# Codes of the last part transposed by DMA, and loads and key parts moved to other tiles, in a quantized cross-attention and FFN kernel

## The chip, the cores and the metric

The kernel runs on one core of one Trainium2 chip. The metric is the device time of one execution in microseconds. Before the change it is 1822.46 us, the median of three runs (1821.18 to 1823.08).

## What is computed

One transformer block on 1600 query rows (16 x 100) of width 512, with a context of 5776 rows (16 x 361): normalized queries, 16 heads of width 32, keys, queries, values and attention weights rounded to 8-bit codes, then a gated FFN of width 1408 whose inputs are rounded row by row. Cut to what matters:

```python
# attention (x is layer-normalized first; B*N = 1600 rows, 5776 keys)
q = (x @ Wq + bq); k, v = split(cond @ Wkv + bkv)
q = fq_sym(q / sqrt(32), axis=-1); k = fq_sym(k, axis=-1); v = fq_sym(v, axis=keys)
attn = softmax(q @ k.T); attn = fq_unsigned(attn, axis=-1)     # codes 0..255 of the row's maximum
x = x + (attn @ v) @ Wp + bp
# FFN
xq = quant_input(layernorm(x))                                  # round(x * 127 / max|x|) per row
x1, x3 = split(xq @ w13.T)
inner = rmsnorm(relu(x1)**2 * x3) * norm_w
x = x + quant_input(inner) @ w2.T
```

## The kernel before

**Stages.** A prologue (to about 145 us) projects the queries, stores their codes in DRAM (`q_dram`) and makes the keys and values of the first four heads. Then come 200 steps, one for each pair of a head and a tile of 128 query rows (the 13th tile, 64 rows high, is shared by two heads, so two heads take 25 steps). Four heads make a group of 50 steps; groups are 0 to 3, and "step 1/35" below means tile 35 of group 1. The last part (from about 1567 us) is the FFN, tile of rows by tile of rows, 13 tiles.

**One step of the attention.** PE multiplies queries by 5776 keys in five chunks (L1247, or L1256 for the shared tile); DVE copies each chunk from PSUM to one of two `score` tiles and takes its maximum (L1263); POOL combines the maxima (L1295, L1306, L1307, which makes the bias `nb`); ACT takes the exponentials in two halves into codes (L1199: `pairc`, `codes`); two DMA transposes on SP's queue turn them (L1204 `pk`, L1207 `rT`); POOL unpacks the first half (L1220); PE multiplies by the values four steps later (L1126). In program order SP gets, in each step, first the `rT` of the step before, then loads, then its own `pk`.

**The plan.** All other work is put by hand into slots of a step with `put(n, slot, fn, ...)`: `pool` (first on POOL in the step), `turn` and `act0` (in one of the windows between chunks), `pe`, `late` (on POOL between the first and the second combination of maxima), `dve` and `act` (after the chunks). The tables `PLAN` (groups 0 to 2) and `LAST` (group 3) give the steps. "keys" holds, for each of the next heads and each part of eight key blocks, the step in which POOL splits it into three bf16 parts (`keys_split`, L368) and the step in which PE turns it (`keys_turn`, L390) and ACT copies it (`keys_keep`, L397); the second head of a group is needed first in step 12 (the shared tile), the third in 25, the fourth in 37 and the next group's first in 50. "query" holds the steps of the three loads of a head's query codes (`query_load`, L403), all three of which a score product needs. "weights" holds the loads and the scalings of four slices of `wp` (L771, L774).

**DMA queues.** Loads in the attention and all transposes are issued by SP; the loads and stores of group 3's partial projections, of the FFN weights (`piece_load`, L461), of `nw_b` (L846) and of the first two residual tiles (`a_load`, L862) by ACT. Each DMA counts on one of eight semaphores, given in turn to the DMAs of SP and ACT in program order.

**The last part.** `START` and then, for each tile t, `EACH` give the order. Each name is a function: `a_turn`, `a_project`, `a_norm`, `a_codes` (codes `hq` of the FFN's input), `a_keep` (four PE transposes into `ph`, one copy to `hT`), `b_up` (16 products for each of three chunks of the 1408), `b_relu`, `b_gate`, `b_codes` (codes `gq` of the inner activations), `b_turn` (eleven PE transposes into `pg` in two calls, copies to `gT`), `b_down` (22 products into `py`), `b_out`. In `EACH` the codes of tile t-1 are made at the start of iteration t, turned in its middle and multiplied in its second half; tile t+1 is prepared in the same iteration. `nw_b` (the norm's weights, 704 KB as they are spread over partitions), the residual tiles `x1_0` to `x1_3` and the other buffers of the last part lie in a ring of memory that in the attention holds the value codes, the key stacks and the queries and keys of the heads (`open_tail`, L829).

## Time and profile before

The profiled execution took 1828.33 us; its profile spans 1826.5 us.

| | us |
|---|---|
| median of the runs | 1822.46 |
| profiled execution, as timed | 1828.33 |
| its span | 1826.5 |
| PE busy | 1630.0 (89%) |
| DVE busy | 1701.5 (93%) |
| ACT busy | 1485.7 (81%) |
| POOL busy | 1321.6 (72%) |

DVE's largest group of instructions is the copy of scores with the maximum (L1263), 1000 times, 1302.1 us. The DMA engines moved 323.87 MB; 87.6% of 16 engines' span went to the queue of the transposes and SP's loads. Busy times are averages over stages; the stages have different limits, so a part of the change is read from its own stage.

In the profile, a row of a timeline gives its start, its duration (both in us), the engine (SPq and ACTq: the DMA issues of SP and ACT), the line, the operation, the tiles written and read, and in brackets the idle time before it and what ended that.

### The profile page before, as it was taken

To read this page: it belongs to the slowest core of one execution; us is meant where nothing else is said; L and a number is where in the kernel's file an instruction comes from. 1 tells how busy PE (TensorE), PEld (TensorE's weight loads), DVE (VectorE), ACT (ScalarE), POOL (GpSimd) and SP (SyncE) were. 2 spreads that over 40 slices of the span, in tenths; PEclk is the share of its full clock that TensorE was granted. 3 is DMA by queue.
4 is the path that set the end of the run, shared out by engine and by line. 5 is a ranking of instruction groups with operands and counts; after the bars stand their busy time and mean duration, and the time that the engine had idled before them with its cause. 6 is when DMAs were issued, how large, how long until landed. Compare 5 with 4: busy or idle time off the path is not lost. (4 is left out here: it accounts for less than half of the span.)

```text
span 1826.5 us, 43719 instructions
## 1 busy us (share of the span) xinstructions
PE 1630.0 (89%) x16745; PEld 1141.9 (63%) x16745; DVE 1701.5 (93%) x2939; ACT 1485.7 (81%) x1471; POOL 1321.6 (72%) x1852
## 2 busy tenths in 40 slices
PE   6999989988888998888889988898898999889998
PEld 6985666656565665565656655655555555568886
DVE  8889999999999998999999999999999999788886
ACT  4656999988899998888999988899889988654443
POOL 5557989877899887778898887889776756542221
PEclk9999999999999999999999999999999999989999
DMA  5646999999999999999999999999999999921000
GB/s 156 161 137 138 202 204 206 207 204 206 195 207 203 202 205 208 198 214 187 201 200 211 207 212 200 201 166 206 198 196 210 210 223 222 185 91 35 24 32 21
DMA packets 982447, 323.87 MB, mean 177 GB/s; under 512 B 939943, under 2 KB 946267, under 8 KB 982238
## 3 DMA queue, kind: packets, MB, share of 16 engines
q1 hardware_dynamic: 970380, 300.91, 87.6%
q10 hardware_dynamic: 11858, 20.18, 4.1%
q8 instruction: 131, 2.15, 0.5%
q14 instruction: 78, 0.64, 0.1%
HBM read 79.16 MB, written 10.72 MB: 49 GB/s over the span
## 5 line engine op out<-in xcount | busy, mean ns | idle before, releaser
L1263 DVE TENSOR_SCALAR_CACHE_REDUCE score<-sl 128x1536 f32<-128x1536 f32 (+1 forms) x1000 | 1302.1, 1354 | 51.8 <-PE sl L1247 35.1
L1247 PE MATMUL sl<-kT,qT 96*128 96x512 bf16 (+1 forms) x2304 | 633.0, 370 | 114.9 <-DVE score L1263 105.7
L1199 ACT ACTIVATE pairc<-score,nb,qs 128x2772 uint8<-128x2772 f32 x192 | 518.4, 2700 | 81.4 <-POOL nb L1307 62.3
L1199 ACT ACTIVATE codes<-score,nb,qs 128x3024 uint8<-128x3024 f32 x192 | 558.2, 2907 | 22.0 <-DMA rT<-codes 20.1
L1220 POOL CAST rU<-pk 128x2816 f16<-128x2816 uint8 x200 | 506.4, 2532 | 7.0 <-DMA pk<-pairc 6.1
L271 PE MATMUL pp<-wkv,cb 128*128 128x256 f32 x1104 | 341.0, 390 | 26.3 <-ACT vraw L294 21.0
L1247 PEld LDWEIGHTS <-qT 96*128 96x128 bf16 x2304 | 183.9, 96 | 208.7 <-issue 139.4
L271 PEld LDWEIGHTS pp<-wkv,cb 128*128 128x128 f32 x1104 | 197.1, 190 | 128.2 <-ACT vraw L294 42.6
L1126 PEld LDWEIGHTS <-rT 128*128 128x128 f16 x4608 | 196.1, 97 | 97.0 <-issue 15.6
L1126 PE MATMUL oacc<-v,rT 128*128 128x32 f16 x4608 | 211.0, 177 | 5.3 <-ACT v L358 1.8
L1306 POOL TENSOR_SCALAR m<-mx,m 128x1 f32<-128x1 f32 x200 | 72.3, 362 | 157.6 <-DVE score L1263 99.9
L1126 PEld LDWEIGHTS <-rU 128*128 128x128 f16 x4224 | 146.1, 96 | 42.6 <-issue 8.2
L1126 PE MATMUL oacc<-v,rU 128*128 128x32 f16 x4224 | 167.5, 177 | 0.0
L957 POOL TENSOR_TENSOR rw<-rl,nw_b 128x480 f32<-128x480 f32 (+3 forms) x39 | 49.1, 1260 | 151.3 <-DVE gq L987 63.6
L939 PE MATMUL p<-w13h,hT 128*128 128x480 f32 (+3 forms) x312 | 122.9, 394 | 1.7 <-ACT hT L924 1.1
L939 PE MATMUL p<-w13l,hT 128*128 128x480 f32 (+3 forms) x312 | 120.9, 387 | 3.5 <-POOL w13l L476 3.3
L399 ACT COPY kT<-kt 96x1008 bf16<-96x1008 bf16 (+2 forms) x97 | 90.7, 935 | 6.6 <-PE kt L395 6.5
L294 ACT COPY vraw<-pp 128x512 f32<-128x512 f32 x92 | 53.1, 577 | 46.8 <-DVE am L283 44.0
L1295 POOL TENSOR_SCALAR m<-mx 128x1 f32<-128x1 f32 x200 | 74.2, 371 | 23.3 <-DVE score L1263 23.1
L311 POOL TENSOR_TENSOR vraw<-vraw,rs 128x256 f32<-128x256 f32 x92 | 59.5, 647 | 40.0 <-DVE rs L306 27.8
L1263 DVE DVE_READ_ACCUMULATOR score<-sl 128x1 f32 x1000 | 82.0, 82 | 0.0
L939 PEld LDWEIGHTS p<-w13h,hT 128*128 128x128 f32 (+1 forms) x312 | 59.4, 190 | 17.0 <-ACT hT L924 7.0
(230 smaller groups left out, 2627.9 us busy)
## 6 DMA issues: line engine op xcount, KB each, us to landing
cb<-in SPq DMA_DIRECT2D x135, 256.0 KB
cr<-in SPq DMA_DIRECT2D x46, 256.0 KB
qT<-q_dram SPq DMA_DIRECT2D x45, 100.0 KB
pk<-pairc SPq DMA_TRANSPOSE x200
rT<-codes SPq DMA_TRANSPOSE x200
xn<-in ACTq DMA_DIRECT2D x12, 256.0 KB
x_s<-in ACTq DMA_DIRECT2D x12, 256.0 KB
x_dram<-x_s ACTq DMA_DIRECT2D x12, 256.0 KB
```

The costliest lines, as they stand in the source:

```text
L271: nc.tensor.matmul(pp, cbs[g, t][:, kb, :], wts_g[g][:, kb, :], start=(kb == 0), stop=False)
L294: nc.scalar.copy(vraw.rearrange("p (u t) c -> p u t c", t=2)[:, u : k + 1 : k - u], pp.rearrange("p t (two c) -> p two t c", two=2),)
L311: nc.gpsimd.tensor_tensor(kv, kv, batch.pop(("rs", g, u)).unsqueeze(3).broadcast_to([P, 2, G, HD]), ALU.mult,)
L399: nc.scalar.copy(kT[h][:, c0 * KB : (c0 + n) * KB].rearrange("p (b k) -> p b k", k=KB), exp_.pop(("pt", h, c0))[:, :n, 2:])
L939: nc.tensor.matmul(pt[:r, :w], T["h", t][:, kb, :r], last_w[c][p][:, i * 4 + kb, :], start=(kb == 0 and p == 0), stop=(kb == 3 and p == 1),)
L1126: nc.tensor.matmul(oacc[h][:, t, :], turned(n, bl), v16[h][:, bl, :], start=(bl == turns[0]), stop=(bl == turns[-1]),)
L1199: nc.scalar.activation(dst, src, AF.Exp, bias=nb, scale=s1, accum_out=usum[:, i, n % 50 : n % 50 + 1])
L1220: nc.gpsimd.tensor_copy(r.rearrange("p (b two) q -> p b two q", two=2), packed.pop(n).bitcast(U8).rearrange("p b (q two) -> p b two q", tw ...
L1247: nc.tensor.matmul(sl[:, x0:x1], qT[h][:, t * P : (t + 1) * P], kT[h][:, col + x0 : col + x1], start=True, stop=True,)
L1263: nc.vector.tensor_scalar(sc[:, col : col + w], sl[:, :w], 1.0, None, ALU.mult, ALU.max, accum_out=mx[:, c : c + 1])
L1295: nc.gpsimd.tensor_scalar(m1, mx[:, 0:1], mx[:, 1:2], mx[:, 2:3], ALU.max, ALU.max)
L1306: nc.gpsimd.tensor_scalar(m2, mx[:, 3:4], mx[:, 4:5], m1, ALU.max, ALU.max)
```

## The change

Four edits. In the last part, the codes `hq` of tiles 4 to 12 and `gq` of tiles 2 to 12 are turned by DMA transposes on SP's queue into new tiles `h16` and `g16`, and ACT copies those to `hT` and `gT`; the subtraction that makes `gq` goes from DVE to ACT as an activation with a bias. `nw_b` is opened and loaded in step 3/36 instead of 3/47, the residual tiles are opened in 3/39, and `x1_0`, `x1_1` are loaded in 3/40 and 3/44 instead of 3/46. The query loads move, and group 3 has its own steps for them. The key parts of the first of group 3's next heads are split and turned sooner, and the scalings of `wp` go from `late` to `pool`.

```diff
@@ PLAN @@
-    "query": ((0, 4, 5), (14, 14, 18), (25, 27, 29), (39, 41, 43)),
+    "query": ((2, 4, 7), (15, 18, 21), (31, 33, 35), (39, 40, 44)),
@@ LAST @@
-        ((-4, 0), (4, 5), (6, 7), (8, 9), (10, 11), (11, 12)),
+        ((-4, 0), (2, 3), (3, 4), (4, 5), (5, 7), (10, 11)),
...
-    "query": ((0, 4, 5), (14, 14, 18), (25, 27, 29)),
+    "query": ((1, 4, 7), (14, 16, 18), (26, 28, 30)),
...
-    "weights": (5, 6, 7, 4, 6, 7, 8, 10),
+    "weights": (4, 5, 6, 4, 6, 7, 8, 12),
@@ open_tail @@
+        def open_norm():
+            T["nw"] = window.tile([P, HID], F32, name="nw_b")
+
         def open_tail():
-            T["nw"] = window.tile([P, HID], F32, name="nw_b")
             T["x1s"] = [window.tile([P, C], F32, name=f"x1_{i}") for i in range(4)]
+
+        def open_rest():
             T["hTs"] = [window.tile([P, 4, P], F32R, name=f"hT_{i}") for i in range(3)]
...
@@ a_codes @@
             nc.vector.tensor_scalar(T["hq"][:r], xn[:r], MAGIC, None, ALU.subtract)
+            if t > FIRST:
+                nc.sync.dma_start_transpose(T["h16"], T["hq"])
             nc.scalar.activation(sd, var, AF.Sqrt, bias=eps_t[:r])
@@ a_keep @@
+            if t > FIRST:
+                hT = T["h", t] = T["hTs"][t % 3]
+                nc.scalar.copy(hT[:, :, :r], T["h16"][:, :, :r])
+                return
@@ b_codes @@
-                nc.vector.tensor_scalar(gq[:r, f0:f1], g[:r, f0:f1], MAGIC, None, ALU.subtract)
+                if t < FIRST - 1:
+                    nc.vector.tensor_scalar(gq[:r, f0:f1], g[:r, f0:f1], MAGIC, None, ALU.subtract)
+                    continue
+                nc.scalar.activation(gq[:r, f0:f1], g[:r, f0:f1], AF.Identity, bias=T["magic"][:r])
+                nc.sync.dma_start_transpose(T["g16"][:, f0 // P : f1 // P, :], gq[:, f0:f1])
@@ b_turn @@
+            if t >= FIRST - 1:
+                b = slice(6 * i, min(6 * i + 6, NF))
+                nc.scalar.copy(gT[:, b, :r], T["g16"][:, b, :r])
+                return
@@ the plan of group 3 @@
-                    put(base + LAST["weights"][4 + kb], "late", weight_scale, kb)
+                    put(base + LAST["weights"][4 + kb], "pool", weight_scale, kb)
...
-                put(base + 46, "act", open_tail)
+                put(base + 36, "act", open_norm)
+                put(base + 36, "act", norm_weights)
+                put(base + 39, "act", open_tail)
+                put(base + 46, "act", open_rest)
...
-                put(base + 47, "act", norm_weights)
-                put(base + 46, "act", a_load, 0)
-                put(base + 46, "act", a_load, 1)
+                put(base + 40, "act", a_load, 0)
+                put(base + 44, "act", a_load, 1)
@@ open_weights @@
+            T["h16"] = wts.tile([P, 4, P], BF16, name="h16")
+            T["g16"] = wts.tile([P, NF, P], BF16, name="g16")
+            T["magic"] = wts.tile([P, 1], F32, name="magic")
+            nc.gpsimd.memset(T["magic"], -MAGIC)
```

## The prediction

> **What bounds the kernel now.** I read the windows first, then the chain of waits, then per-engine timelines. A step below is one of the 200 query tiles of the attention; step 1/35 is tile 35 of group 1 (50 tiles, four heads each).

> The windows (span; then busy time of PE, PEld, DVE, ACT, POOL; granted clock; DMA share; GB/s):

> ```profile
> 600.00:1000.00 400.00, 353.87 (x4166) 239.55 (x4164) 384.95 (x634) 363.37 (x305) 338.50 (x501) 0.99 1.10 203
> 1643.00:1660.20 17.20, 17.20 (x90) 14.12 (x89) 15.22 (x34) 8.13 (x18) 3.80 (x3) 1.00 0.10 31
> ```

> In the attention (145 to 1567 us) DVE is busy 96% and the DMA engines are full: two limits of nearly one size. In the last part (from 1643 us) one tile takes 17.20 us and PE never pauses; DMA is at 0.10. The chain of waits there:

> ```profile
> 1660.20 0.91 PE po L884 x2
> 1661.11 6.99 PE p L939 x32
> 1668.10 0.63 PE pg L996 x11
> 1668.73 3.29 PE p L939 x16
> 1672.13 5.02 PE py L1005 x22
> 1677.15 0.24 PE ph L921 x4
> ```

> Those six rows add up to the period. `pg` and `ph` are the transposes that the change takes off PE.

> **Part 1, transposes by DMA.** PE loses 0.63 us in the ten iterations that turn tiles 2 to 11 and 0.24 us in the nine that turn tiles 4 to 12: 6.3 + 2.2 = 8.5 us, from a stage where PE is the bound. DVE loses two subtractions (L987, 0.56 + 1.39 us a tile). ACT gains them as activations of 768 and 640 elements; the rows nearest are ACT's 480-wide relu (0.66 us) and its 1024-wide copy (1.00), so some 0.8 + 0.75. ACT is busy 8.13 of 17.20, so it has room, but it works in order. SP gains three issues a tile; the prologue's `q16T` transpose, 128x512 like `h16`, issues in 1.20 us and lands 2.4 to 5.2 us after its start (start of L612 to the L613 that waits for it, 13 times, median 2.9). I take 2.9 for all three; the 640- and 768-wide ones may be a little longer.

> Do they fit into a period of 17.2 - 0.87 = 16.3? Times from the start of the tile's first `p`: the first scaled half of `g` is done at 2.8 (old trace), ACT's activations end at 3.7 and 4.5, SP issues at 3.7 and 4.9, the halves land at 6.6 and 7.8. ACT comes to its copies only after L968 of the first chunk, at 9.0, and ends them at 10.4; PE wants the first at 6.99 + 3.29 + 0.1 = 10.4. `hq` was ready at 11.95, now some 0.5 sooner: landed 14.4, copied 15.0, wanted at 16.3. So both are covered, by about a microsecond each. Queued behind ACT's new waits are the first relu (2.6 us later, with its POOL product hidden under `p`) and the last L968 before the next scaling; SP's loads of x1 stand behind two issues, 2.4 us, and are used two tiles later.

> At the end nothing covers. Old: first multiply done 1814.77, `py` starts 1817.29, 2.5 us. New: 0.8 + 2.9 + 0.48 (the 128x384 copy) + 0.15 = 4.3, so +1.8. Before it the last relu stands behind copies that now end 1.5 us later than its `p`. Part 1: -8.5 + 3.3 = **-5.2 us**. Bounds: landing at 5.2 puts `hT` at 17.2, the old period, so no gain and +6 at the end; landing at 2.4 gives -6.

> [...]

> **Part 2, norm weights and residuals.**

> ```profile
> 1556.75 0.34 ACTq L846 DMA_DIRECT2D nw_b<-in  x1
> 1557.21 2.70 ACT L1199 ACTIVATE pairc<-score,nb,qs 128x2772 uint8<-128x2772 f32 x1 [6.92 <-DMA rT<-codes]
> 1560.03 1.23 DVE L1263 TENSOR_SCALAR_CACHE_REDUCE score<-sl 128x1024 f32<-128x1024 f32 x1 [2.73 <-ACT pairc L1199]
> ```

> At step 3/47 ACT stands 6.92 us before the issue of `nw_b`, which (by the program's semaphores, eight used in turn by all DMAs) waits for the transpose eight DMAs back. DVE loses 2.73 us to it. In step 3/36 the eighth DMA back is a `pk` transpose two steps old: no wait. ACT's last exponentials also come sooner. I take **-3.0 us**; bounds -6 (ACT's whole wait) and 0 (704 KB and twice 256 KB now meet the transposes in steps 36 to 44; at 205 GB/s 704 KB are 3.4 us, which the 2 us lag of the transposes there must swallow).

> **Part 3, key parts of the last group.** Step 3/12 waits for the last part and takes 9.10 us where 6.5 to 6.7 is usual; 3/13 takes 8.89 at a granted clock of 0.74:

> ```profile
> 1303.52 1.22 DVE L1263 TENSOR_SCALAR_CACHE_REDUCE score<-sl 128x1024 f32<-128x1024 f32 x1 [1.49 <-PE sl L1256]
> ```

> One step earlier, the turn removes up to 4.5 us there and perhaps 1 at 3/8, where three `weight_scale` (1.59 us each) no longer stand between the two maxima on POOL. Against it: POOL in steps 3/2 and 3/3 is already full with the value divisions (6.65 and 7.7 us); each gets a split of 2.85 us more (L382 to L388, 1242.88 to 1245.73 on POOL), ahead of the unpacking and the maxima. Followed through POOL, ACT and DVE, `nb` of step 3/3 comes 6 us later and DVE stands 4 to 5 us in step 3/5, since `pairc` must have read the score tile. I take **-0.4 us**, -5 to +5.

> **Part 4, query loads.** All stand on SP, behind the transposes. SP in group 1, and the PE row that opens step 1/37, the first to need head 3's queries:

> ```profile
> 751.75 3.83 SPq L1207 DMA_TRANSPOSE rT<-codes  x1
> 755.66 0.53 SPq L249 DMA_DIRECT2D cb<-in  x1
> 756.29 1.54 SPq L1204 DMA_TRANSPOSE pk<-pairc  x1
> 757.93 0.79 SPq L434 DMA_DIRECT2D v<-row  x1
> 758.83 4.29 SPq L1207 DMA_TRANSPOSE rT<-codes  x1
> ...
> 763.23 0.62 PE L1256 MATMUL sl<-kT,qT 96*64 96x512 bf16 x4
> ```

> SP works without a gap and a step behind: the transpose at 758.83 is that of step 34 (its codes ended at 755.8). The third load of (31, 33, 35) comes right behind it. In the old order all three lay ahead; now two do, so that transpose ends 0.6 us sooner whatever DVE does, at 406.5, 762.5 and 1119.0 in the three groups. Landing: `cb` loads issued at that place landed 3.2 and 3.5 us later (issues 1057.45 and 1043.05, PE released 1060.66 and 1046.59), a 1.5 KB load 2.2 us later. With 2.8 and 0.75 us of PE before DVE starts, step 37 starts at 410.1, 766.1, 1122.6 instead of 407.6, 764.8, 1120.3: **+6.2 us**, any gain before it included, since SP and not DVE sets it. Bounds: 2.2 gives +4.4, 5.2 (the slowest `cb`, 372.13 to 377.30) +13. What speaks for the move: the loads leave steps 25 to 29, where late `cb` loads stop PE; steps 25 to 33 run over their usual times by 2.0, 4.9 and 3.7 us. The other loads land steps before use; I cost them at nothing (lag of at most 8 us against three steps).

> **Sum:** -5.2 - 3.0 - 0.4 + 6.2 = -2.4 us on the profiled 1826.5 us span (1828.3 as timed, 5.9 above the median of 1822.46). Carried to the median: 1820.

> **Rivals.** (A) The loads of step 35 land in time, because SP runs further ahead than I think. Then part 4 gives back about half of the 10.6 us above: -5.2 - 3.0 - 0.4 - 5 = -13.6, 1809. For: those stalls are in the trace. Against: no gap on SP. Chance 0.25. (B) PE's pause at step 37 lowers its clock, as in step 1/30, which took 9.61 us at 0.82 behind a 0.64 us wait. Place: the three steps 37 and 38; price about 3 us each, so -2.4 + 9 = +6.6, 1829; it decides once the pause is as long as that in 3/12 (1.17 us, clock 0.88 then 0.74). Against: the 1.94 us wait at 377.3 left the clock up. [...] Chance 0.25. (C) Transposes in the last part land 5 us late: part 1 becomes +6, sum +8.8, 1831. Against: 12 of 13 `q16T` did better than 5. Chance 0.08. (D) The forecast, 0.42, its own range 1815 to 1826.

> **Numbers.** About 0.2%, 3.6 us, can be told from no change. Faster: A and 0.17 of D, 0.42. Slower: C, 0.20 of B and 0.05 of D, 0.33. Same: the rest, 0.25. Range 1807 to 1832, A's and C's sums with a little room.

> **What will show it.** Right: period 16.3 us after 1640 with no PE wait; `nw_b` issued near step 3/36 with no ACT wait; PE at the first L1256 of steps 37 waiting for `qT`. Wrong: PE waiting for `hT` or `gT` copies each tile; no `qT` wait; DVE unbroken in 3/5.

## The result, and the profile after

The changed kernel takes 1838.58 us in the median of four runs (1832.07 to 1839.58); the kernel before, beside it, takes 1822.37. The ratio is 1.0072, 95% interval 1.0047 to 1.0096: some 13 us slower, with 9 to 17 as its bounds. (The two medians alone differ by 16.2 us; the text goes by the ratio.) A second measurement, 11 runs, gave 1.0060 (1.0037 to 1.0083). The forecast was 1820 and its range ended at 1832: it was wrong, and wrong in sign.

The page of the changed kernel, its span and the busy time of PE and DVE:

```profile
span 1836.6 us, 43474 instructions
PE 1628.1 (89%) x16588; PEld 1137.4 (62%) x16588; DVE 1690.2 (92%) x2917; ACT 1503.4 (82%) x1493; POOL 1320.2 (72%) x1853
```

PE and DVE are busy for less time than before (1628.1 against 1630.0, 1690.2 against 1701.5 us), and the span is 10.1 us longer: the loss is waiting, not work. (PE's busy time also counts products at the half clock: in the 6.82 us from 406.70, at a granted 0.50, PE counts as busy for all 6.82.) The windows of the same two stretches as before (busy time of PE, PEld, DVE, ACT, POOL; granted clock, which is PE's clock as a share of its full speed; DMA share; GB/s):

```profile
600.00:1000.00 400.00, 353.72 (x4110) 237.40 (x4110) 381.12 (x628) 359.51 (x302) 334.47 (x495) 0.98 1.08 200
1660.03:1676.25 16.22, 16.22 (x75) 13.54 (x74) 13.43 (x33) 10.24 (x23) 3.57 (x3) 1.00 0.25 64
```

The last part does what was forecast: a tile takes 16.22 us where it took 17.20, PE still without a pause. The attention loses: DVE is busy 381.12 of 400 us where it was 384.95. The chain of waits in the last part has lost its `pg` and `ph` rows, and ends on a transpose by DMA (2.56 us) and 22 products of 7.63 us at a mean granted clock of 0.67, where the 22 at 1670.38 take 5.01 at 1.00:

```profile
1660.03 10.24 PE p L949 x48
1670.38 5.01 PE py L1023 x22
1675.39 0.86 PE po L888 x2
...
1821.75 2.56 DMA g<-gq
...
1824.95 7.63 PE py L1023 x22
```

Where the time went was found by taking the start of DVE's first copy of each of the 200 steps in both profiles. Steps 36 and 37 of the first three groups together took 14.99, 15.01 and 14.99 us before; now they take 19.93, 22.13 and 22.55. That is 19.6 us, more than the whole loss. Group 0, on SP and then on PE:

```profile
399.52 4.20 SPq L1227 DMA_TRANSPOSE rT<-codes  x1
403.78 0.58 SPq L407 DMA_DIRECT2D qT<-q_dram  x1
```

```profile
403.79 0.38 PE L1276 MATMUL sl<-kT,qT 96*64 96x512 bf16 x1
406.33 0.74 PE L1276 MATMUL sl<-kT,qT 96*64 96x512 bf16 x3 [2.16 <-DMA qT<-q_dram]
...
765.78 1.06 PE L1276 MATMUL sl<-kT,qT 96*64 96x512 bf16 x3 [2.61 <-DMA qT<-q_dram]
...
1130.57 1.06 PE L1276 MATMUL sl<-kT,qT 96*64 96x512 bf16 x3 [3.35 <-DMA qT<-q_dram]
```

The third query load is issued behind the transpose of the step before and lands 2.55 us later; PE waits 2.16, 2.61 and 3.35 us for it. So far this is the forecast's part 4. But DVE, in step 0/37, stands still four times and not once:

```profile
407.18 1.22 DVE L1283 TENSOR_SCALAR_CACHE_REDUCE score<-sl 128x1024 f32<-128x1024 f32 x1 [1.75 <-issue]
409.76 1.76 DVE L1283 TENSOR_SCALAR_CACHE_REDUCE score<-sl 128x1536 f32<-128x1536 f32 x1 [1.35 <-PE sl L1276]
412.20 1.22 DVE L1283 TENSOR_SCALAR_CACHE_REDUCE score<-sl 128x1024 f32<-128x1024 f32 x1 [0.67 <-issue]
414.27 1.76 DVE L1283 TENSOR_SCALAR_CACHE_REDUCE score<-sl 128x1536 f32<-128x1536 f32 x1 [0.84 <-PE sl L1276]
```

The first wait is the landing, the other three are a PE that comes too late with its scores. (Two of the rows end on "issue", for which the profile names no releaser; that these too wait for PE is read from the windows below, in which PE is never idle behind the pause.) The windows say why (PE busy is the second number, the granted clock the third from the end):

```profile
399.87:403.29 3.42, 3.37 (x41) 2.44 (x40) 3.42 (x5) 3.42 (x4) 3.27 (x5) 1.00 1.09 165
403.29:406.70 3.41, 1.14 (x7) 0.33 (x5) 2.14 (x6) 2.14 (x3) 2.17 (x5) 1.00 0.99 212
406.70:410.11 3.41, 3.41 (x15) 1.66 (x13) 1.58 (x3) 3.41 (x3) 3.23 (x4) 0.50 0.85 178
410.11:413.52 3.41, 3.41 (x21) 1.70 (x22) 2.65 (x4) 1.00 (x2) 0.08 (x1) 0.50 1.08 205
413.52:416.94 3.42, 3.42 (x52) 2.13 (x49) 2.67 (x5) 0.00 (x0) 0.37 (x1) 1.00 0.91 182
```

Behind the pause the granted clock is 0.50 for 6.8 us, and PE is busy without a gap: it has become the bound. In groups 1 and 2 the half clock lasts 13.7 and 10.2 us. The profile of before has no such stretch at any step 36 or 37.

The whole span, from rows of the two profiles: at the start of step 3/49 the changed kernel is 12.6 us behind, at the first full tile of products (1660.03 against 1643.92) 16.1, at the half tile (1805.52 against 1798.68) 6.8, and at the end 10.1. So the nine periods give 9.3 back, and the stretches before and after them take 3.5 and 3.3. What took the 3.5 was not followed.

### The profile page after: what moved, and what is told of

The parts are those of the page before. It is cut to its first block, busy times and chain, and to the rows that moved or that the text cites. A ratio compares the mean times of both kernels' runs of the same rounds, so it can differ in the third digit from the quotient of the medians.

```text
span 1836.6 us, 43474 instructions
## 1 busy us (share of the span) xinstructions
PE 1628.1 (89%) x16588; PEld 1137.4 (62%) x16588; DVE 1690.2 (92%) x2917; ACT 1503.4 (82%) x1493; POOL 1320.2 (72%) x1853
## 5 line engine op out<-in xcount | busy, mean ns | idle before, releaser
L1240 POOL CAST rU<-pk 128x2816 f16<-128x2816 uint8 x200 | 506.2, 2531 | 10.9 <-DMA pk<-pairc 9.2
L271 PE MATMUL pp<-wkv,cb 128*128 128x256 f32 x1104 | 347.0, 396 | 22.7 <-ACT vraw L294 18.0
L395 PEld LDWEIGHTS <-stack 128*96 128x96 bf16 x736 | 54.2, 124 | 27.0 <-POOL stack L388 6.8
```

Of the source, the lines that this page charges most:

```text
L271: nc.tensor.matmul(pp, cbs[g, t][:, kb, :], wts_g[g][:, kb, :], start=(kb == 0), stop=False)
L1240: nc.gpsimd.tensor_copy(r.rearrange("p (b two) q -> p b two q", two=2), packed.pop(n).bitcast(U8).rearrange("p b (q two) -> p b two q", tw ...
```

## The experiments

The theory from here on: part 4 costs the whole loss and more, a third of it by the late landing and two thirds by the clock that PE's pause brings down. Its rivals: that the loss lies in the other parts, that moving the loads crowds SP wherever they stand, and that the later waits are PE's put-off work rather than its clock. Each run was timed against the kernel before on its own chip, so that ratios are compared; 0.1% is 1.8 us. "Steps 36 and 37" are the two steps together, in the first three groups, from the profile.

**1. The new query loads undone** (both rows back to before):

```diff
-    "query": ((2, 4, 7), (15, 18, 21), (31, 33, 35), (39, 40, 44)),
+    "query": ((0, 4, 5), (14, 14, 18), (25, 27, 29), (39, 41, 43)),
-    "query": ((1, 4, 7), (14, 16, 18), (26, 28, 30)),
+    "query": ((0, 4, 5), (14, 14, 18), (25, 27, 29)),
```

> The changed kernel with the query loads of before, all else changed. Theory (the late third load is the loss): the three pairs of steps 36 and 37, which cost 4.9, 7.1 and 7.6 us over before in the profile, are as before again, and the cb stalls in steps 25 to 33 are back (some 2 to 5 us in all): 1838.6 - 19.6 + 2..5 = 1821 to 1824, about the kernel before. No wait of PE for qT, no stretch of half clock at steps 37. Rival (the loss lies in the other parts, the query loads cost the 6.2 us of my forecast): 1831 to 1833.

Measured: 1819.91 us, ratio 0.9970 (0.9957 to 0.9984); steps 36 and 37 take 14.99, 14.99 and 15.00 us. The other three parts together are a gain of about 5.5 us.

**2. The new query loads alone** (the same two edits, made to the kernel before).

> The kernel before with the new query loads alone. Theory: 1822.4 + 19.6 - 2..5 = 1837 to 1840. Rival (the term is the 6.2 us of my forecast and the rest of the loss comes from the other parts): 1828 to 1830. With the run that undoes this part it also tells whether the parts add up.

Measured: 1847.65 us, ratio 1.0106 (1.0087 to 1.0125), +19.3 us; steps 36 and 37 take 20.30, 21.47 and 21.30 us, 18.1 over before. Runs 1 and 2 agree: the loss is part 4, and it is not 6.2 us.

**3. Only the third load a step sooner:**

```diff
-    "query": ((2, 4, 7), (15, 18, 21), (31, 33, 35), (39, 40, 44)),
+    "query": ((2, 4, 7), (15, 18, 21), (31, 33, 34), (39, 40, 44)),
```

> The changed kernel with the third query load at step 34 instead of 35 in the first three groups; the other loads stay moved. Theory (only this one load is late, by 1.8 to 3.3 us at DVE): one step is 7.4 us, so it lands 4 us and more before its use, steps 36 and 37 take 7.4 and 7.6 us, and the gains in steps 25 to 33 stay: 1838.6 - 18..20 = 1818 to 1821. Rival (moving the loads as such crowds SP, wherever the third one stands): no more than a third of that comes back, 1832 or more.

Measured: 1821.53 us, ratio 0.9971 (0.9956 to 0.9987); steps 36 and 37 take 14.99, 15.00 and 14.98 us. One load, one step, is the whole of the loss. The hoped gain from clearing steps 25 to 29 is not there: with the loads of before (run 1) the ratio is the same.

**4. PE kept busy while it waits,** ahead of the scores of a step's first chunk (these products are extra, and their result is overwritten):

```diff
+                if c == 0 and n in (37, 87, 137):
+                    for _ in range((10, 12, 14)[n // 50]):
+                        nc.tensor.matmul(sl[:, 0:512], ident_b[0 : 3 * HD, :], kT[h][:, 0:C], start=True, stop=True)
```

> The changed kernel with 10, 12 and 14 more 512-column products put ahead of the scores of steps 37 of the three groups, into the tile that these scores then overwrite: PE is busy while it waits for qT, the load lands as late as before. Theory (the half clock after the pause is the larger part of the loss): no clock drop there, the later waits in these steps (2.9, 4.2 and 3.9 us) vanish, DVE still loses 1.8, 2.5 and 3.3 us to the landing: 1838.6 - 11 = 1827 to 1829. Rival (the later waits are the backlog of PE's own work, which the pause has put off, and not the clock): 1837 to 1841.

Measured: 1827.31 us, ratio 0.9995 (0.9976 to 1.0015). The timeline of PE in step 0/37 of this kernel, and its windows:

```profile
407.02 2.32 PE L1266 MATMUL sl<-kT,ident_b 96*128 96x512 bf16 x10
409.27 0.40 PE L1279 MATMUL sl<-kT,qT 96*64 96x512 bf16 x1
409.90 0.62 PE L1279 MATMUL sl<-kT,qT 96*64 96x512 bf16 x3 [0.23 <-DMA qT<-q_dram]
```

```profile
405.41:408.83 3.42, 3.26 (x23) 1.79 (x21) 3.27 (x8) 2.15 (x3) 2.17 (x5) 1.00 1.14 203
408.83:412.24 3.41, 3.18 (x20) 1.33 (x19) 1.45 (x3) 3.41 (x3) 3.23 (x5) 1.00 1.03 235
```

The load lands as late as before, the ten products fill the pause, the clock stays at 1.00, and PE's own work waits about as long as it did. Steps 36 and 37 now take 17.34, 17.48 and 17.56 us: 7.4 us over before instead of 19.6. So 12.2 us were the clock and 7.4 the landing; the rival of the put-off work falls. The 7.4 is an upper bound for the landing: in group 2 the load is issued at 1125.46 and should land by 1128.1 (an estimate from the 2.4 to 2.6 us of the changed kernel), and the fourteen products end only at 1128.67. In time, the ratio falls by 0.0077 from the first measurement of the changed kernel (14 us) and by 0.0065 from the second (12 us).

**5. The third load at its late place, but from ACT** (`late` is true for the loads at step 35):

```diff
-            (nc.sync if live else nc.scalar).dma_start(
+            (nc.sync if live and not (late and r == 2) else nc.scalar).dma_start(
```

> The changed kernel with the third query load at step 35 as it is, but issued by ACT instead of SP, in the first three groups. Theory (the load is late since SP is a step behind, not since a load of step 35 is too late as such): ACT comes to it some 5 us before SP does, at the end of step 35, it lands before step 37, steps 36 and 37 take 15.0 us and the time is that of the kernel with the third load at step 34: ratio 0.997, 1820. Rival (the transfer itself is slow beside the transposes): PE still waits for qT and the ratio is over 1.002.

Measured: 1810.78 us, ratio 0.9948 (0.9925 to 0.9972); steps 36 and 37 take 14.99, 15.00 and 15.00 us. ACT's issues in group 0:

```profile
396.47 0.34 ACTq L407 DMA_DIRECT2D qT<-q_dram  x1
```

The same load of the same step is issued at 396.47 from ACT and at 403.78 from SP. What made it late is the queue in which it stood. Its interval overlaps that of run 3, so no gain of ACT over an earlier load is claimed.

**6. The transposes of the last part alone** (the edits of `a_codes`, `a_keep`, `b_codes` and `b_turn`, and their three tiles, in the kernel before).

> The kernel before with the transposes of the last part by DMA alone. Theory: from the start of step 3/49 to the end of the span the four profiles with this part so far take 264.0, 260.8, 267.5 and 261.0 us, the two without it 266.5 and 268.1: -4.0 us against the kernel before; the period of a full tile is 16.2 us instead of 17.2 (9.3 us over nine tiles), the last chain 1.7 us longer, and the rest is given back by the clock at the last products. Forecast of the record: -5.2. Rival (what the periods give, the end and the clock take back in full): within 1.5 us of the kernel before.

Measured: 1816.24 us, ratio 0.9955 (0.9932 to 0.9978), -8.2 us. The profiles give -4.9: from the start of step 3/49 to the end, the four profiles with the old last part average 267.9 us, and the nine with the new one (run 11 left out) 262.9. The rival falls.

**7. The norm's weights and the residuals alone** (the moved `put` rows of the buffers and loads and the split `open_tail`, in the kernel before).

> The kernel before with the loads of the norm's weights and of the residuals alone moved. Forecast of the record: -3.0 us, by the stall of DVE in step 3/48. Rival: no gain, 0 to +2 us; the stall is not in every run (the profile with the query loads alone has steps 3/44 to 3/49 at 33.9 us without the move, where that of before has 36.6), and the four profiles with the move take 44.3, 42.3, 43.5 and 44.9 us for steps 3/38 to 3/43 against 41.4 and 43.0 without it.

Measured: 1821.45 us, ratio 0.9984 (0.9963 to 1.0004). That is -2.9 us with nothing inside the interval, and run 10 shows no gain when it is added: inconclusive.

**8. The key parts and the weights' scaling alone** (the `keys` and `weights` rows of the last group and "late" to "pool").

> The kernel before with the key parts of the last group and the scaling of the projection's weights alone moved. Theory: steps 3/0 to 3/9 take 72.4 us instead of 68.2 (DVE waits in steps 3/4 and 3/5 for PE, whose clock then drops), steps 3/10 to 3/19 take 69.8 instead of 74.4, sum -0.4 us as in the forecast, time within 1.5 us of the kernel before. Rival (one of the two is chance of the clock): -4 or +4 us.

Measured: 1825.92 us, ratio 1.0010 (0.9991 to 1.0028), +1.8 us. Steps 3/0 to 3/9 take 72.90 us and 3/10 to 3/19 71.49; over the seven profiles with the new keys as they are in the change the means are 72.4 and 70.1, over the six with the old ones 68.1 and 73.5. A loss of 4.3 and a gain of 3.4, which nearly cancel. The loss stands in every profile (71.7 us and more against 69.4 and less); the gain only in the means, since the two sets overlap (68.8 to 71.5 against 70.7 to 75.0).

**9. Keys late again, but for the last two** (on the kernel of run 3):

```diff
-        ((-4, 0), (2, 3), (3, 4), (4, 5), (5, 7), (10, 11)),
+        ((-4, 0), (4, 5), (6, 7), (8, 9), (9, 10), (10, 11)),
```

> The changed kernel with the third query load at step 34 and with the key parts of the last group as late as before, but for the last two, each a step sooner. Theory: the loss in steps 3/0 to 3/9 is gone (68 us instead of 72) and the gain in steps 3/10 to 3/19 stays (70 instead of 74): 4 us under the kernel with the third load at step 34 alone, 1817.5 where the kernel before takes 1826.5. Rival (splits on POOL in steps 3/6 to 3/9 only move the loss): the same time as that kernel, 1821.5.

Measured: 1819.23 us, ratio 0.9984 (0.9966 to 1.0002): no gain. Steps 3/0 to 3/9 do fall to 68.0 us, but step 3/10 alone takes 16.36, with one wait of DVE of 7.92 us: the splits of two parts now follow each other on POOL, and PE stands 6.71 us for ACT's copy of turned keys into `kT`. The expectation was wrong; the stall was moved.

**10. The last part and the norm together** (runs 6 and 7 in one kernel).

> The kernel before with the transposes of the last part by DMA and with the moved loads of the norm's weights and residuals; keys and queries as before. Theory: the two gains add up, -8.2 - 2.9 = -11 us, ratio 0.994, under both kernels. Rival (the norm's gain is within its interval and is nothing): ratio 0.9955.

Measured: 1812.85 us, ratio 0.9953 (0.9929 to 0.9977). Faster than both kernels, and no better than the last part alone.

**11. The same, with PE kept busy before the last tile's products:**

```diff
+            if t == NT - 1:
+                for _ in range(14):
+                    nc.tensor.matmul(py, ident_b, T["h16"].rearrange("p b q -> p (b q)"), start=True, stop=True)
```

> The same as the run with the last part and the norm, with 14 products of 512 columns ahead of the last tile's 22 products, into the tile that these overwrite, so that PE is busy while it waits for the last transpose. Theory (the clock): the 22 products take 5.0 to 5.3 us and not 6 to 7.6, no stretch of half clock begins in the last 16 us: 1 to 2.5 us less than without them, which only the profile can tell apart. Rival (the products themselves hold the last tile up): the last product starts over 4.5 us after the tile before it ends.

Measured: 1807.83 us, ratio 0.9921 (0.9894 to 0.9949). The end of the chain of waits, first without the extra products (run 10), then with them:

```profile
1800.73 2.55 DMA g<-gq
1803.36 0.52 ACT gT L1008
1803.92 7.66 PE py L1023 x22
```

```profile
1796.61 3.18 PE py L1023 x14
1799.80 5.15 PE py L1026 x22
```

The 22 products take 5.15 us instead of 7.66. The granted clock is 0.50 from 1802.27 to 1809.09 us in run 10 and 1.00 through all of these products in run 11: 2.5 us come from the clock. They start 4.27 us after the tile before ends its products, against 4.24, so the extra products hold nothing up. (The medians differ by 5 us, but the intervals overlap, and from the start of step 3/49 to the end this profile takes 261.9 us, that of run 10 260.6: the 2.5 us are shown for these products and not for the whole.) Its ratio is the lowest of all runs, 14 us under the kernel before, but the intervals of runs 5, 6 and 10 overlap it.

**12. The changed kernel once more,** unedited.

> The changed kernel once more, beside the kernel before on this chip. Theory: the parts add up; measured alone they give -8.2 (last part), -2.9 (norm), +1.8 (keys) and +19.3 us (queries), sum +10.0, so a ratio of 1.0055, and steps 36 and 37 of the first three groups take 20 to 22.5 us together. Rival (the parts disturb each other): the ratio of its first measurement, 1.0072 or more.

Measured: 1834.78 us, ratio 1.0060 (1.0037 to 1.0083), against 1.0055 from the parts alone, so the parts add up within the interval, which also holds the 1.0072 of the first measurement. Steps 36 and 37 take 22.76, 22.74 and, in group 2, only 16.69 us. That odd one is an experiment that nobody planned. The windows of group 1 (the first two rows) and of group 2:

```profile
764.00:767.41 3.41, 1.02 (x5) 0.42 (x4) 2.39 (x6) 2.14 (x3) 2.17 (x6) 1.00 1.03 207
767.41:770.83 3.42, 2.50 (x10) 1.20 (x12) 1.23 (x2) 3.42 (x3) 3.24 (x4) 0.50 1.05 240
...
1125.81:1129.23 3.42, 2.33 (x17) 1.36 (x15) 3.42 (x8) 2.48 (x2) 2.29 (x3) 1.00 1.23 163
1129.23:1132.64 3.41, 2.46 (x16) 1.30 (x17) 1.90 (x4) 3.08 (x3) 3.11 (x6) 1.00 0.94 218
1132.64:1136.05 3.41, 3.41 (x42) 2.01 (x40) 3.41 (x5) 2.60 (x2) 2.04 (x2) 1.00 0.94 178
```

In group 1 PE pauses for 3.19 us (765.14 to 768.33), of which 2.3 lie in one window; PE is busy 1.02 us of it and the clock halves. In group 2 a pause of 1.88 us lies across the border of two windows, half in each; each is busy 2.3 us and more, and the clock stays at 1.00. There the late load costs 1.7 us over before (16.69 against 14.99), which the pause alone covers. The second pause is shorter too, so this pair alone doesn't tell place from length.

## Why the prediction was wrong

**The step that failed** is the last of part 4 and rival B together: "the three steps 37 and 38; price about 3 us each", put at a chance of 0.25 because "the 1.94 us wait at 377.3 left the clock up". The pauses were in the forecast; that they cost nothing beyond themselves was the error. Behind the pauses of 2.16, 2.61 and 3.35 us the granted clock was 0.50 for 6.8, 13.7 and 10.2 us, and the price was 12.2 us over three groups (run 4), 4 and not 3 each. The wait at 377.3 was weak evidence: it lies in a window (375.69 to 379.10) in which PE was busy for 1.81 of 3.41 us. Of the 11 windows with 1.8 to 1.9 us in all the profiles (the last section has the counts), 8 were followed by the half clock; this one is among the other three. Rival B, as written, was right that the pause lowers the clock, but its 1829 was too low as well.

**Part 4, landing:** right in its mechanism and nearly in size. PE waits for `qT` in the named row of the three steps; forecast +6.2, measured 7.4 at most. The forecast said that SP would set the time of the issue whatever DVE gained before; in group 0 SP issued the load 2.7 us sooner (403.78 for a forecast 406.5), and it landed in 2.4 to 2.6 us in the three groups, for a forecast 2.8. What I hoped for from the emptied steps 25 to 29 (rival A's give-back) is not in runs 1 and 3. The forecast read it off one profile: steps 25 to 33 of the first three groups take 198.4 us in the profile of before, but 193.2 in the mean of the six other profiles with the old loads, and 194.3 in that of the seven with the new ones. Whole part: forecast +6.2 with bounds of 4.4 to 13, measured +19.3 (15.9 to 22.8).

**Part 1:** right. The period is 16.22 us for a forecast 16.3. The last chain: the tile before ends its products at 1820.71 and the last `py` starts at 1824.95, 4.2 us for a forecast 4.3. Those last 22 products then take 7.63 us for 5.30, at a granted clock of 0.50 up to 1830.06 us and 0.67 in the mean (1.00 before), which the forecast lacks. Sum: forecast -5.2, measured -8.2 (-12.4 to -4.0) in time and -4.9 in the profiles. Rival C did not come.

**Part 2:** the wait went as described. `nw_b` is now issued in the middle of ACT's work, and the exponentials after it start without a wait:

```profile
1487.03 1.20 ACTq L850 DMA_DIRECT2D nw_b<-in  x1
...
1488.34 2.70 ACT L1219 ACTIVATE pairc<-score,nb,qs 128x2772 uint8<-128x2772 f32 x1
```

The stall is gone: step 3/48, which takes 9.21 us before, takes 6.50 in all ten profiles with the moved loads. With the old loads it takes 9.35 and 8.41 (runs 6 and 8) and 6.50 in run 2, where ACT still stands 4.27 us but DVE loses nothing. Whether the move is worth the forecast -3.0 stays open: -2.9 alone with zero in the interval, nothing on top of part 1, and steps 3/36 to 3/48 together take 92.0 us in the mean of the four profiles with the old loads and 93.4 in that of the ten with the moved ones (90.8 to 93.0 and 90.1 to 97.6). So the forecast's bound of no gain, where the loads meet the transposes in the steps before, is not ruled out.

**Part 3:** right in sum (forecast -0.4, measured +1.8, -1.6 to 5.1) and, in the means of run 8, in its two halves. The loss came a step sooner and by another way than mine through `nb`. In the changed kernel PE's transposes of the keys wait for a split that stands behind 4.02 us of value divisions on POOL, and DVE waits for PE:

```profile
1260.19 1.09 PE L395 MATMUL kt<-ident_b,stack 128*96 128x128 bf16 x8 [3.49 <-POOL stack L388]
```

```profile
1262.90 1.76 DVE L1283 TENSOR_SCALAR_CACHE_REDUCE score<-sl 128x1536 f32<-128x1536 f32 x1 [4.03 <-PE sl L1267]
```

DVE stands 4.03 us, for a forecast of 4 to 5. The parts alone sum to -8.2 - 2.9 + 1.8 + 19.3 = +10.0 us; the changed kernel is 13.1 and 10.9 us slower in its two measurements.

## What to carry to other kernels

A load's step in a plan is not the time of its issue: place it by the queue. Here the same load of step 35 was issued at 403.78 us from SP, behind the transpose of the step before, and at 396.47 from ACT (run 5), where a step takes some 7.5 us. A pause of PE in a stage that PE nearly fills (353.72 of 400 us here) is to be priced twice, once as itself and once as the slow clock behind it; here the first was 7.4 us at most and the second 12.2. Where the pause can't be removed, try products that nobody needs, put in front of the waiting one: 10, 12 and 14 of them took the second price away in run 4. And a stall that one profile shows may be that execution's own (step 3/48 took 9.21, 9.35 and 8.41 us in three profiles with the old loads and 6.50 in the fourth): look for it in a second one before it is counted as a gain.

## What the runs showed of the hardware

| PE busy of 3.41 us | windows | next window at half clock |
|---|---|---|
| under 1.8 us | 70 | 69 |
| 1.8 to 2.4 us | 522 | 61 |
| over 2.4 us | 6399 | 6 |

So in these traces the half clock also follows windows in which PE was busy for half of the time (61 of the 522 with 1.8 to 2.4 us), and not only idle ones. Of the 217 windows at half clock, none of the 47 in which PE was busy under 2.9 us ended the half clock, and 136 of the other 170 did. These are counts from fourteen executions of this kernel and its variants; what makes them was not shown. What decides between 1.8 and 2.4 us, and why 34 windows with PE busy for 2.9 us and more did not bring the clock back, stays open.

In run 12 the late load of one and the same kernel costs 1.7 us in group 2 and 7.7 in group 1, with pauses of 1.88 and 3.19 us. Whether the place of a pause on the grid counts there, beside its length, was not shown. The kernel before takes 1816.82 to 1833.55 us on one chip (beside runs 6 to 9), a spread of 17 us; whether the clock is its cause was not tested.
